# A four-layer graph network on one core: d added on TensorE for two tiles of five, norms ended on ScalarE, one scale product on GpSimd, and a new table of places

## The chip, the core and the metric

The kernel runs on one core of a Trainium2 chip. The core has TensorE (PE, matrix products into PSUM), VectorE (DVE), ScalarE (ACT), GpSimd (POOL) and SyncE (SP, which here issues the DMAs). Each engine runs its own instructions in the order in which they were issued; semaphores between the engines keep the dependencies. The metric is the device time of one execution, in microseconds (us).

## The reference

There are 64 graphs of 256 nodes with 128 features, and a 0/1 adjacency matrix for each. Four layers follow one another, each as x = layernorm(x + layer(x, adj)):

```python
# layer 0: p = x @ (W1 - W2), q = x @ W2
x0 = max over j of relu(p_i + q_j + b) * adj[i, j]
# layer 1: three elu projections, two aggregations adj @ . and adj.T @ ., tanh update
# layer 2: a graph convolution with normalised adjacency, elu between its products
# layer 3, for every edge i, j:
pre = m_j + m_i + b1                    # m_j = x @ W1[:D], m_i = x @ W1[D:]
msg = gelu(layernorm(pre) * g1 + be1)
agg_i = sum over j of msg * adj[i, j]
updated = layernorm(concat(x, agg) @ W2 + b2) * g2 + be2
```

Layer 3 is the large one: a normalised, gated message for each edge.

## The kernel before, in words

**Sparse edges as columns.** The kernel sorts the nodes of a graph by their number of neighbours and lays the neighbours out in 40 slots (`RECTS`). Slot s is a block of columns, one for each node that may have an s-th neighbour; all slots together are `WIDTH` = 4800 columns for each half of the nodes. `hot` is a 0/1 matrix (fp8) that picks for every column which of the half's 128 nodes is its neighbour, so that one product `c3 x hot` on TensorE gathers the neighbours' part of the message into columns. The features are split into three bf16 parts (`split3`), hence three products for each block of 512 columns.

**Tiles of layer 3.** `TILES` cuts the 4800 columns of a half into four tiles of 1024 columns and one of 704; with both halves there are ten tiles in a graph (`TODO`). Tiles 0 to 2 hold whole slots of 256 columns. For each tile `sums_of` (L855) does the following. TensorE makes blocks of 512 columns in PSUM. VectorE adds the receiving node's part `dT`, repeated for every slot, and writes `pre` in SBUF. ScalarE squares `pre` into `sq`, TensorE sums the squares over the partitions with a matrix of ones, ScalarE scales them into `row`. A DMA writes the row to a `line` in DRAM; for two tiles at a time, it is read back as 128 x 16 (`vr`), GpSimd raises it to the power -1/2 and multiplies it by the mask `fu`, and DMAs write it to DRAM and spread it over all partitions (`rs_s`). `last` (L960) then multiplies `pre` by `rs_s` on VectorE, applies Gelu with scale and bias on ScalarE, and adds the tile to `sums` on VectorE (`fold`). A product with a part of W2 follows for each half, and `update` (L436) adds, normalises and stores. `sums_of` runs four tiles ahead of `last` (`AHEAD`); `pre` has 7 buffers, `rs_s` 3, `sq` 1.

**Norms.** `layernorm` (L296) is used five times in a graph: at the end of layers 0, 1 and 2 (x1, x2, x3), for y of layer 3, and for the output. VectorE takes mean and variance (`bn_stats`, `bn_aggr`), GpSimd adds epsilon and raises to -1/2 (`rs`, two instructions), and VectorE ends it: for each half one `tensor_scalar` (subtract the mean, multiply by rs), or, with gamma and beta, two `scalar_tensor_tensor`. In layers 0 to 2 TensorE transposes the result next.

**Order.** Nothing in the program is a loop on the chip. A tape (`Tape`, L86) records the instructions of each graph, in four parts (`first`, `second`, `third`, `last`). `AT` gives each of the 665 recorded instructions of a graph a place, and graph g stands g x `PERIOD` later; all instructions of all graphs are issued in the order of `AT[i] + g * PERIOD`. So several graphs are in work at once, and an engine meets their instructions in the order that the table gives, not in the order in which their inputs become ready. `BANKS` gives the PSUM bank of each of the 82 PSUM tiles of a graph. In the profile almost every instruction has line L117, the place where the tape plays it, so groups are told apart by tile names.

Of the kernel before, what the change touches and what calls it, by code (L numbers as in the profile page):

```python
# [9 lines left out]
F32 = mybir.dt.float32  # L10
# [18 lines left out]
for _s0, _n, _w in RECTS:  # L29
# [10 lines left out]
PERIOD = 68597  # L40
AT = [
    0, 17760, 60075, 113136, 105182, 105182, 105183, 102831, 102831, 102831, 110669, 110669, 110669, 110669,
    106819, 106819, 106819, 106819, 132589, 112770, 113194, 113191, 114149, 114680, 115572, 116600, 127108, 127385,
    127477, 127638, 128456, 128456, 128456, 128456, 129252, 167352, 167352, 167352, 167352, 170028, 167469, 167469,
    167469, 167469, 169266, 129252, 129869, 138338, 138338, 175384, 175384, 175384, 175384, 185704, 188498, 198206,
    138877, 158428, 163223, 205266, 194576, 218329, 202165, 190466, 198713, 197410, 172321, 133325, 134073, 132100,
    134755, 130433, 131857, 138013, 130475, 132679, 141029, 136544, 147371, 141091, 138254, 149904, 142022, 143828,
    134350, 136963, 130888, 154057, 152143, 136812, 131597, 135682, 150302, 50267, 50267, 51142, 106173, 106173,
    110809, 113092, 114103, 115412, 142716, 142716, 142716, 142716, 142716, 138772, 138772, 138772, 138772, 138772,
    146600, 143243, 143243, 143243, 143243, 143243, 148201, 146140, 146140, 146140, 146140, 146140, 150206, 145880,  # L50
    145880, 145880, 145880, 145880, 151986, 151684, 151684, 151684, 151684, 151684, 152911, 152448, 152448, 152448,
    152448, 152448, 156338, 153971, 153971, 153971, 153971, 153971, 153971, 153971, 153971, 157134, 157697, 157805,
    157380, 157380, 157380, 157380, 157380, 157380, 157380, 157380, 158172, 158547, 160090, 143916, 143916, 143916,
    143916, 157893, 161048, 162139, 172702, 172702, 172702, 161211, 161211, 161211, 161211, 165106, 163675, 163675,
    163675, 163675, 163675, 165268, 165091, 165091, 165091, 165091, 165091, 166836, 165893, 165893, 165893, 165893,
    165893, 167925, 166285, 166285, 166285, 166285, 166285, 168867, 150182, 150182, 150182, 150182, 150182, 170700,
    170268, 170268, 170268, 170268, 170268, 171887, 172059, 172059, 172059, 172059, 172059, 172059, 172059, 172059,
    173999, 174804, 175613, 174543, 174543, 174543, 174543, 174543, 174543, 174543, 174543, 176934, 178826, 179479,
    163756, 163756, 163756, 163756, 164398, 179873, 180116, 180116, 180116, 182699, 182699, 182699, 182699, 182699,
    182699, 182699, 182699, 182699, 182699, 182699, 182699, 182699, 182699, 182699, 182699, 182699, 184638, 186829,  # L60
    188393, 190261, 192462, 189659, 192419, 192462, 192463, 193382, 193799, 194283, 194283, 196229, 197739, 197739,
    197863, 199404, 199404, 199767, 196229, 196269, 196428, 198141, 203643, 204759, 204759, 204759, 204759, 204759,
    207105, 207105, 207105, 207105, 207105, 207105, 209069, 209905, 209982, 211997, 213309, 211020, 212716, 216020,
    216021, 216021, 216021, 138164, 164455, 180398, 183224, 195565, 216021, 216021, 216232, 217871, 217871, 219655,
    220859, 221353, 222845, 224313, 225709, 225758, 226367, 227329, 227329, 227329, 227329, 227488, 229896, 229896,
    230186, 230112, 230186, 232038, 233437, 234508, 235780, 235780, 235780, 235780, 235780, 237440, 238099, 238099,
    238277, 238100, 239978, 240898, 243374, 241359, 243047, 244102, 247526, 247526, 248324, 188591, 248522, 248522,
    248522, 249117, 249117, 252769, 251596, 251704, 253761, 254891, 252769, 252769, 252769, 252769, 256816, 257931,
    257931, 257931, 257931, 256055, 256055, 256055, 256994, 258732, 260232, 260232, 260232, 260232, 260803, 260803,
    259203, 259203, 259203, 260422, 259088, 259088, 259088, 259089, 260678, 261279, 261279, 261279, 261279, 261442,  # L70
    261696, 270059, 272065, 277752, 279128, 279128, 261244, 261244, 261244, 261305, 260228, 260228, 260228, 260814,
    261622, 262731, 262731, 262731, 262731, 266778, 275218, 263270, 263270, 263270, 265037, 259210, 259210, 259210,
    261433, 263668, 268962, 270855, 270855, 270855, 270855, 271063, 277538, 279564, 285260, 296203, 296203, 296203,
    281115, 285903, 260489, 260489, 260489, 270476, 264721, 266934, 268118, 268118, 268118, 271078, 272421, 274438,
    274438, 274438, 274438, 280012, 286089, 283767, 291651, 298416, 268002, 268002, 268002, 271712, 268406, 268406,
    268406, 273881, 277066, 281788, 281788, 281788, 281788, 282305, 292280, 296324, 283720, 296324, 301082, 308174,
    285903, 292378, 303270, 266792, 266792, 266792, 269082, 269338, 269338, 269338, 271169, 282084, 284789, 284789,
    284789, 284789, 288190, 302392, 300082, 305371, 310143, 296586, 292360, 292360, 292360, 296407, 290067, 290067,
    290067, 295222, 296579, 298916, 298916, 298916, 298916, 299552, 306172, 309408, 304155, 309648, 314896, 315843,
    305620, 308455, 311827, 306236, 301007, 301007, 301007, 302221, 296040, 296040, 296040, 301658, 297892, 306172,  # L80
    308294, 308294, 308294, 308294, 308659, 310486, 315715, 316106, 317663, 313660, 317279, 318829, 305328, 305328,
    305328, 309145, 308304, 308057, 304348, 304348, 304348, 308422, 313472, 314786, 314786, 314786, 314786, 314858,
    317455, 319233, 325254, 326737, 326737, 327338, 319719, 321478, 324328, 320137, 320749, 323171, 320164, 327517,
    331173, 331173, 331173, 331173, 331173, 331173, 331173, 331173, 331173, 331173, 331173, 331173, 331173, 323787,
    324347, 327390, 324328, 329258, 327518, 324432, 329492, 329598, 330030, 330250, 331498, 331262, 332381, 333437,
    333711, 335099, 336414, 335343, 337991, 342336, 342336, 342336, 342336, 342336, 342336, 342336, 342336, 342336,  # L86
    342336, 342336, 342336, 342337, 350509, 350509, 350509, 350509, 350509, 350509, 350509, 350509, 350509, 350509,
    354346, 357521, 365298, 358477, 367762, 370480, 370480, 372624, 382049, 380501, 380733, 384069, 386653, 390490,
    389663, 400076, 408707, 408708, 420847, 415132, 436409,
]  # L90
BANKS = [
    3, 0, 0, 5, 0, 4, 2, 7, 1, 7, 5, 4, 3, 5, 7, 0, 2, 7, 3, 0, 5, 1, 4, 3, 7, 0, 3, 1, 6, 7, 1, 2, 5, 6, 2, 2, 4,
    6, 7, 2, 3, 5, 7, 4, 7, 0, 3, 1, 3, 6, 0, 2, 4, 1, 0, 6, 5, 1, 5, 7, 4, 3, 0, 4, 1, 6, 0, 2, 5, 4, 2, 4, 0, 2,
    1, 1, 3, 5, 6, 4, 3, 6,
# [73 lines left out]
def kernel(  # L168
# [118 lines left out]
    class Shared:  # L287
# [8 lines left out]
        def layernorm(self, dst, src, at, g=None, be=None):  # L296

            st = self.work.tile([P, H, 6], F32, name="st_" + at, bufs=2)
            mv = self.work.tile([P, H, 2], F32, name="mv_" + at, bufs=2)
            for h in range(H):  # L300
                nc.vector.bn_stats(st[:, h], src[:, h])
                nc.vector.bn_aggr(mv[:, h], st[:, h])
            rs = self.work.tile([P, H], F32, name="rs_" + at, bufs=2)
            nc.gpsimd.tensor_scalar(rs, mv[:, :, 1], EPS, 1.0, ALU.add, ALU.mult)
            inverse_root(rs)
            yield
            for h in range(H):
                if g is None:
                    nc.vector.tensor_scalar(
                        dst[:, h], src[:, h], mv[:, h, 0:1], rs[:, h:h + 1], ALU.subtract, ALU.mult  # L310
                    )
                else:
                    nc.vector.scalar_tensor_tensor(dst[:, h], src[:, h], mv[:, h, 0:1], g, ALU.subtract, ALU.mult)
                    nc.vector.scalar_tensor_tensor(dst[:, h], dst[:, h], rs[:, h:h + 1], be, ALU.mult, ALU.add)
# [159 lines left out]
    def sparse(ctx):  # L474
# [306 lines left out]
        def layer_0(s):  # L781
# [66 lines left out]
            yield from sh.layernorm(s["x1"], y, "0")  # L848

        TODO = [(h, t0, tl) for h in range(H) for t0, tl in TILES]  # L850
        AHEAD = 4
        GROUP = 2
        PIECE = 16

# [428 lines left out]
```

## Time and profile before

| | |
|---|---|
| time, median of 3 runs | 4605.34 us (4604.03 to 4610.56) |
| the profiled execution's own time | 4603.78 us |
| its span | 4601.9 us |
| granted TensorE clock, mean | 0.957 |
| DMA | 365.10 MB, mean 79 GB/s |
| square of `pre` on ScalarE, 128x1024 | 512 times, 1052 ns |
| sums over slots on VectorE, 128x1024 | 256 times, 1213 ns |
| power of `vr` on GpSimd, 128x16 | 192 times, 2942 ns |

How to read it: PE is TensorE's matmuls, PEld its weight loads, which overlap them. "x" with a number is a count of instructions. A group's row has the tile that is written, the tiles that are read, the forms, the count, the busy time in us, the mean length of one in ns, and after the second bar the idle time ahead of these instructions on their engine with what ended it. Busy times of overlapping instructions are counted once, so busy divided by count can be less than the mean length. In the windows view, each row has the start, end and length of a stretch and each engine's busy time in it. In the view of waits a row is: the waiting engine and tile, what it waited for, total us, times, longest. In the chain and the timeline the first two numbers are start and length in us.

### The profile page before, as it was taken

The numbers are of one execution on the slowest core, as the hardware profiler recorded it, in microseconds if no ns is written. First come the engines' busy times: TensorE is split into PE (matmuls) and PEld (weight loads), VectorE is DVE, ScalarE is ACT, GpSimd is POOL, SyncE is SP. The second block draws the span as 40 slices with busy tenths as digits, with TensorE's granted clock in tenths as the row PEclk, the third lists the DMA queues.
The fourth block names the chain that finished last, engine by engine and source line by source line (L and its number), as shares of the span: only waits on it lengthen the run. The fifth ranks groups of instructions, "written<-read, shape, count | busy, mean of one in ns | idle before, by whom it ended". The sixth has DMA issues, their size and how long they took to land.

```text
span 4601.9 us, 83551 instructions
## 1 busy us (share of the span) xinstructions
PE 4000.7 (87%) x28434; PEld 2519.0 (55%) x28434; DVE 4467.9 (97%) x12373; ACT 2967.6 (64%) x4862; POOL 1848.6 (40%) x1674
## 2 busy tenths in 40 slices
PE   4889889889889888898898898898888988988985
PEld 2555555555555555555555555555555555555553
DVE  6999999999999999999999999999999999999997
ACT  2666666666666666666666666666666666666664
POOL 0344343434444444443444434444444434344443
PEclk9999999999999999999999999999999999999997
DMA  1122222222222222222222222222222222222222
GB/s 28 62 84 77 82 81 80 76 89 81 77 80 80 85 77 85 85 77 82 80 81 76 89 81 76 81 80 84 81 81 85 77 82 80 81 76 89 78 72 94
DMA packets 292663, 365.10 MB, mean 79 GB/s; under 512 B 151936, under 2 KB 210304, under 8 KB 292224
## 3 DMA queue, kind: packets, MB, share of 16 engines
q1 hardware_dynamic: 292224, 359.66, 24.5%
q8 instruction: 225, 3.69, 0.3%
q14 instruction: 214, 1.75, 0.1%
HBM read 345.00 MB, written 14.53 MB: 78 GB/s over the span
## 4 chain that ended last, share of the span: by engine, by line
DVE 62%; PE 28%; issue 7%; ACT 2%; DMA 1%; POOL 1%; SPq 0%; DVEq 0%; POOLq 0%; ACTq 0%
PE ps L117 28%; DVE pre L117 18%; DVE lanes L117 12%; DVE sums L117 10%; DVE hot L117 4%; DVE hs L117 3%; DVE x L117 2%; DVE st L117 2%; DVE z L117 2%; DVE io L117 2%; DVE perm L117 1%; DVE elu_hs L117 1%; DVE mv L117 1%; DVE total_m L117 1%; ACT row L117 1%
## 5 line engine op out<-in xcount | busy, mean ns | idle before, releaser
L117 POOL TENSOR_TENSOR vr<-vr,mhalf 128x16 f32<-128x16 f32 (+1 forms) x320 | 994.3, 3107 | 451.0 <-DMA vr<-line 451.0
L117 PE MATMUL ps<-hot,q 128*128 128x512 fp8e4 (+1 forms) x3840 | 922.8, 365 | 58.6 <-ACT row L117 52.9
L117 POOL TENSOR_SCALAR rs<-mv 128x2 f32<-128x2 f32 x256 | 134.4, 525 | 2003.4 <-DVE mv L117 2003.3
L117 PE MATMUL ps<-hot,c 128*128 128x512 fp8e4 (+1 forms) x3840 | 892.1, 366 | 0.9 <-ACT row L117 0.9
L117 DVE TENSOR_TENSOR pre<-ps,dT 128x512 f32<-128x512 f32 (+6 forms) x1664 | 857.4, 532 | 6.1 <-PE ps L117 2.7
L117 ACT ACTIVATE sq<-pre 128x1024 f32<-128x1024 f32 (+1 forms) x640 | 640.1, 1000 | 336.4 <-DVE pre L117 282.4
L117 DVE TENSOR_TENSOR lanes<-ps,lanes 128x512 f32<-128x512 f32 (+6 forms) x1536 | 767.1, 499 | 3.5 <-ACT lanes L117 1.0
L117 DVE TENSOR_TENSOR pre<-pre,rs_s 128x1024 f32<-128x1024 f32 (+1 forms) x640 | 734.7, 1148 | 10.3 <-DMA rs_s<-scale_line 10.2
L117 ACT ACTIVATE pre<-pre,be,g 128x1024 f32<-128x1024 f32 (+1 forms) x512 | 600.5, 1173 | 105.3 <-DVE pre L117 101.3
L117 DVE TENSOR_TENSOR sums<-pre,sums 128x1024 f32<-128x1024 f32 (+6 forms) x1024 | 631.0, 616 | 0.4 <-ACT pre L117 0.2
L117 PEld LDWEIGHTS <-c 128*128 128x128 bf16 x3840 | 353.2, 98 | 347.7 <-issue 70.2
L117 DVE TENSOR_SCALAR hot<-rank 128x512 fp8e4<-128x512 bf16 (+5 forms) x1536 | 503.5, 355 | 1.5 <-ACT rank L117 1.4
L117 PEld LDWEIGHTS <-q 128*128 128x128 bf16 x3840 | 322.3, 97 | 300.5 <-issue 94.6
L117 PE MATMUL ps<-sq,ones 128*32 128x256 f32 (+1 forms) x5120 | 392.7, 378 | 54.2 <-ACT sq L117 51.7
L117 PEld LDWEIGHTS <-pick 128*128 128x128 bf16 x2944 | 240.1, 97 | 258.3 <-issue 1.4
L117 ACT ACTIVATE row<-ps,eps_t 128x256 f32<-128x256 f32 (+1 forms) x640 | 290.8, 454 | 126.3 <-PE ps L117 124.5
L117 ACT ACT_TABLE_LOAD x253 | 324.6, 1283 | 22.6 <-DVE w3c L117 18.2
L117 PE MATMUL ps<-w3u,sums 128*128 128x128 f32 x2048 | 287.4, 287 | 28.3 <-DVE sums L117 17.1
L117 PE MATMUL ps<-ident,x 128*128 128x128 f32 x512 | 137.5, 325 | 198.2 <-DVE x L117 189.5
L117 PEld LDWEIGHTS ps<-w3u,sums 128*128 128x128 f32 x2048 | 251.7, 193 | 80.1 <-DVE pre L117 36.2
L117 PE MATMUL ps<-lack,pick 128*128 128x6 bf16 (+16 forms) x2944 | 266.1, 185 | 0.0
L117 POOL TENSOR_TENSOR rs<-rs,mhalf 128x2 f32<-128x2 f32 x256 | 249.8, 976 | 16.1
(230 smaller groups left out, 7357.0 us busy)
## 6 DMA issues: line engine op xcount, KB each, us to landing
rs_s<-scale_line SPq DMA_DIRECT2D x512, 512.0 KB
rs_s<-scale_line SPq DMA_DIRECT2D x128, 352.0 KB
an<-in_adj SPq DMA_DIRECT2D x64, 256.0 KB
x<-in_x SPq DMA_DIRECT2D x64, 128.0 KB
line<-row SPq DMA_DIRECT2D x512, 4.0 KB
out<-o SPq DMA_DIRECT2D x64, 128.0 KB
vr<-line SPq DMA_DIRECT2D x192, 8.0 KB
fu<-fulls SPq DMA_DIRECT2D x192, 4.0 KB
```

The source lines that it names most:

```text
L117: getattr(getattr(self.nc, engine), op)(*args, **named)
```

## The change

- For tiles 1 and 2 of each half (`OWN`), d is added on TensorE: after the three products of a 512 block, four transposing products with `dk` as stationary matrix and the identity as moving one are accumulated into the same bank. ScalarE then copies the bank to `pre`, where VectorE added before. `dk` is the transpose of `dT`, made once for each graph by four transposes and one ScalarE copy.
- For tile 3 of each half (`SLOW`) the product `pre` times `rs_s` is on GpSimd instead of VectorE.
- `layernorm` ends on ScalarE: GpSimd makes `off` = -mean x rs in two instructions, and for each half one Identity activation with scale rs and bias off follows. The form with gamma and beta is gone: for y of layer 3, VectorE multiplies by gamma (one 128x256 product), and beta is added to x3 beforehand on GpSimd (`x3b`).
- `AT` has 712 places for 712 instructions, `BANKS` 83, and `PERIOD` is 76270 instead of 68597.

```diff
-PERIOD = 68597
+PERIOD = 76270
...
-        def layernorm(self, dst, src, at, g=None, be=None):
+        def layernorm(self, dst, src, at):
...
             for h in range(H):
-                if g is None:
-                    nc.vector.tensor_scalar(
-                        dst[:, h], src[:, h], mv[:, h, 0:1], rs[:, h:h + 1], ALU.subtract, ALU.mult
-                    )
-                else:
-                    nc.vector.scalar_tensor_tensor(dst[:, h], src[:, h], mv[:, h, 0:1], g, ALU.subtract, ALU.mult)
-                    nc.vector.scalar_tensor_tensor(dst[:, h], dst[:, h], rs[:, h:h + 1], be, ALU.mult, ALU.add)
+            off = self.work.tile([P, H], F32, name="off_" + at, bufs=2)
+            nc.gpsimd.tensor_tensor(off, mv[:, :, 0], rs, ALU.mult)
+            nc.gpsimd.tensor_scalar(off, off, -1.0, 0.0, ALU.mult, ALU.add)
+            yield
+            for h in range(H):
+                nc.scalar.activation(
+                    dst[:, h], src[:, h], AF.Identity, bias=off[:, h:h + 1], scale=rs[:, h:h + 1]
+                )
...
+            x3b = self.work.tile([P, H, P], F32, name="x3b")
+            nc.gpsimd.tensor_tensor(x3b, x3, over_halves(be3u), ALU.add)
...
-            yield from self.layernorm(z, y, "3", g3u, be3u)
-            nc.vector.tensor_add(z, z, x3)
+            yield from self.layernorm(z, y, "3")
+            nc.vector.tensor_mul(z, z, over_halves(g3u))
+            nc.vector.tensor_add(z, z, x3b)
...
+        OWN = (TILE, 2 * TILE)
+        SLOW = (3 * TILE,)
...
                     nc.tensor.matmul(
-                        pt[:, :bl], c3[:, k, h], hot[:, h, t0 + b:t0 + b + bl], start=k == 0, stop=k == 2
-                    )
+                        pt[:, :bl], c3[:, k, h], hot[:, h, t0 + b:t0 + b + bl],
+                        start=k == 0, stop=k == 2 and not own,
+                    )
+                if own:
+                    for o in range(0, 512, P):
+                        nc.tensor.matmul(
+                            pt[:, o:o + P], dk[:, h, o // P % H], ident, start=False, stop=o + P == 512,
+                            is_transpose=True,
+                        )
+                    nc.scalar.copy(pre[:, b:b + 512], pt)
+                    continue
...
+            pk = psum()
+            for h in range(H):
+                for hk in range(H):
+                    cols = slice((h * H + hk) * P, (h * H + hk + 1) * P)
+                    nc.tensor.transpose(pk[:, cols], dT[:, h, hk * P:(hk + 1) * P], ident)
+            dk = state.tile([P, H, H, P], F32, name="dk")
+            nc.scalar.copy(dk.rearrange("p a b d -> p (a b d)"), pk)
...
-                    nc.vector.tensor_mul(pre[:, :tl], pre[:, :tl], rs[:, :tl])
+                    if t0 in SLOW:
+                        nc.gpsimd.tensor_tensor(pre[:, :tl], pre[:, :tl], rs[:, :tl], ALU.mult)
+                    else:
+                        nc.vector.tensor_mul(pre[:, :tl], pre[:, :tl], rs[:, :tl])
```

The two tables are left out of this diff. Where each instruction falls on its engine follows from sorting the places modulo the period.

## The prediction, made before the changed kernel ran

> **What bounds the kernel now.** I read the page's busy shares and its chain first, then a stretch of the steady state, then single groups. Busy shares and chain:
>
> ```profile
> PE 4000.7 (87%) x28434; PEld 2519.0 (55%) x28434; DVE 4467.9 (97%) x12373; ACT 2967.6 (64%) x4862; POOL 1848.6 (40%) x1674
> DVE 62%; PE 28%; issue 7%; ACT 2%; DMA 1%; POOL 1%; SPq 0%; DVEq 0%; POOLq 0%; ACTq 0%
> ```
>
> VectorE (DVE) is nearly full, but TensorE (PE) stands close behind it. The windows of the middle, and one piece of the chain that returns with every graph:
>
> ```profile
> core 0: us, PE busy (x) PEld busy (x) DVE busy (x) ACT busy (x) POOL busy (x), PEclk, DMA share, GB/s
> 1700.00:2400.00 700.00, 621.55 (x4445) 391.62 (x4444) 692.44 (x1911) 463.87 (x760) 288.74 (x261) 0.96 0.26 81
> 2040.11 11.48 PE ps L117 x99
> 2180.06 11.48 PE ps L117 x99
> ```
>
> Two graphs take 2180.06 - 2040.11 = 139.95, so one takes 69.98 us. Of this DVE is busy 69.24 (98.9%), PE 62.16, ScalarE (ACT) 46.4, GpSimd (POOL) 28.9. 64 x 69.98 = 4479 of the span of 4601.9; the other 123 are filling and draining. The profiled execution took 4603.8, the median of the runs is 4605.3; I work on 4603.8.
>
> **DVE, per graph.** The groups by form that lose work, and the one nearest to what is added:
>
> ```profile
> L117 DVE TENSOR_TENSOR pre<-pre,rs_s 128x1024 f32<-128x1024 f32 x512 | 621.9, 1215 | 10.3 <-DMA rs_s<-scale_line 10.2
> L117 DVE TENSOR_TENSOR pre<-ps,dT 128x512 f32<-128x512 f32 x896 | 598.5, 681 | 5.7 <-PE ps L117 2.7 <-ACT sums L117 1.6 <-ACT dT L117 1.2
> L117 DVE TENSOR_SCALAR x<-hs,mv,rs 128x128 f32<-128x128 f32 x128 | 96.5, 754 | 0.0
> L117 DVE TENSOR_SCALAR x<-y,mv,rs 128x128 f32<-128x128 f32 x256 | 77.0, 344 | 6.6 <-POOL rs L117 1.9
> L117 DVE SCALAR_TENSOR_TENSOR z<-z,rs,be3u 128x128 f32<-128x128 f32 x128 | 43.0, 338 | 1.0 <-POOL rs L117 0.8
> L117 DVE SCALAR_TENSOR_TENSOR z<-y,mv,g3u 128x128 f32<-128x128 f32 x128 | 41.7, 326 | 0.0
> L117 DVE TENSOR_SCALAR o<-z,mv_o,rs_o 128x128 f32<-128x128 f32 x128 | 41.1, 323 | 1.1 <-POOL rs_o L117 1.1
> L117 DVE TENSOR_TENSOR z<-z,x 128x256 f32<-128x256 f32 x64 | 27.2, 424 | 0.0
> ```
>
> I divide the busy column by 64 graphs. The d additions: 8 of 14 are gone, 598.5 x 8/14 / 64 = 5.34. The scale products of the fourth tile: 2 of 8, 621.9 / 4 / 64 = 2.43. The norms' ends: (96.5 + 77.0 + 43.0 + 41.7 + 41.1) / 64 = 4.68. Added is one product by gamma, 27.2 / 64 = 0.42. DVE: 69.24 - 12.45 + 0.42 = 57.2 us. The old end of layer 2's norm shows that POOL can hold it up:
>
> ```profile
> 2009.89 1.15 POOL L117 TENSOR_TENSOR diff<-an,nz 128x512 bf16<-128x512 f32 x1
> 2009.91 1.22 DVE L117 TENSOR_SCALAR x<-hs,mv,rs 128x128 f32<-128x128 f32 x1
> 2011.17 0.33 DVE L117 TENSOR_SCALAR x<-hs,mv,rs 128x128 f32<-128x128 f32 x1
> ```
>
> The same instruction takes 0.33 alone and 1.22 beside a POOL product: 0.89 of the 1.15 is lost. The new products are twice as long, 2 x 1.157 = 2.3 us, twice per graph. [...] I take 0.77 (0.89/1.15) of it, 3.6, since sums and products with two inputs fill much of that stretch: DVE 60.8. Either way (57.2 to 61.8) it is no longer the fullest.
>
> **PE.** Added are 32 transposes that add d and 4 that make dk. Rows of the same instruction with the same operands' shape (layer 2 adds hs so):
>
> ```profile
> 2058.66 0.81 PE L117 MATMUL ps<-aT,hs 128*128 128x256 f32 x3
> 2059.30 0.38 PE L117 MATMUL ps<-ident,hs 128*128 128x128 f32 x2
> 2059.52 0.81 PE L117 MATMUL ps<-hot,c 128*128 128x512 fp8e4 x3
> ```
>
> Two of them hold PE for 2059.52 - 2059.30 = 0.22, so 0.11 each: 36 x 0.11 = 4.0 us. The group's busy time (48.9 us for 256) would say 0.19, or 6.9. [...] The rows' 273 ns is a duration with its pipeline latency in it, not a distance; I take 0.11. Weight loads hide behind the matmul before (PEld 55%). PE: 62.2 + 4.0 = 66.1. [...]
>
> **ACT.** The rows to price from:
>
> ```profile
> L117 ACT COPY lanes<-ps 128x512 f32<-128x512 f32 x128 | 73.2, 572 | 15.5 <-DVE total_m L117 9.1 <-PE ps L117 6.4
> L117 ACT ACTIVATE pre<-pre,be,g 128x1024 f32<-128x1024 f32 x384 | 475.8, 1239 | 11.6 <-DVE pre L117 10.6
> L117 ACT ACT_TABLE_LOAD x253 | 324.6, 1283 | 22.6 <-DVE w3c L117 18.2
> ```
>
> Nine copies of 128x512 (eight d blocks, one dk): 9 x 0.57 = 5.1. Ten norm ends of 128x128 with both scale and bias from memory: Gelu at 1024 takes 1239 and at 704 takes 974, so 0.83 ns an element and 0.39 fixed, 0.50 at 128; a 128x176 row takes 0.41. I take 0.45: 4.5. The table of places puts Gelu, Tanh and Exp in another order: sorted modulo its period there are six changes between Gelu and the others, where the old table has four (253 / 64), so 2 x 1.28 = 2.6. ACT: 46.4 + 12.2 = 58.6.
>
> **POOL and queues.** Two products 4.6, five "off" products at 0.71 (the row dinv by pos), five negations at 0.52 (rs from mv), x3b 0.6 (half of diff): 28.9 + 11.4 = 40. No bound, but order matters: POOL's second product now stands right before layer 0's rs, and waits for its scale DMA; rs, and behind it ACT's norm end and PE's transposes of x1, wait with it. DMAs are the same in number and size; only SP's order is new. x3b costs nothing while POOL idles; in a full POOL it would be its 0.6.
>
> **Sum.** Fullest is now PE, 66.1, against 69.98: at most 3.9 us a graph to gain. What PE still waits for decides. Today:
>
> ```profile
> PE ps L117 <- DVE x L117: 189.5, 129, 3.4
> PE ps L117 <- DVE hs L117: 107.6, 248, 2.2
> ```
>
> With the smaller ones that name DVE (pre 23.2, total_m 20.7, sums 17.1, io 13.9, perm 13.2) this is 385 us, 6.0 a graph; waits that name ACT (row 53.7, sq 51.7, nzp 22.9, x3T 17.1) are 145, 2.3 a graph. A DVE at 60.8 of 68 no longer has a standing queue, so I drop the 6.0 and keep ACT's 2.3: 66.1 + 2.3 = 68.4 a graph. Filling and draining get longer by five norms of 1.4 (below) and dk, 8 us. 4603.8 - 64 x 1.6 + 8 = 4509; I say **4510**, with 4440 to 4590 for this case alone.
>
> **Rivals.**
> - *PE never waits* (14%). 66.1 a graph: 4603.8 - 64 x 3.9 + 8 = 4362. For it: DVE and ACT both under 61. Against: three engines now stand within 8 us of each other and all run in a fixed order.
> - *The norm is the new wait* (30%, slower). A norm's end was POOL 0.52 + 0.98, then DVE. Now POOL does two more instructions (0.71 + 0.52), and ACT takes it 0.2 slower than DVE: 1.4 longer; behind it in ACT's order stand the copies that free PSUM. POOL's rs takes 0.19 to 1.33 today, depending on DVE, so the added pair may cost 0.4 to 2.6. x1, x2 and x3 stand before PE: 3 x 1.4 = 4.2 a graph if the new order puts no other PE work there. 66.1 + 2.3 + 4.2 = 72.6: 4603.8 + 64 x 2.6 + 8 = 4778. It decides once PE idles over 3.9 us a graph. If the old 3.0 for x stays beside it, 75.6 and 4971. For it: waiting for x is PE's largest wait already.
> - *Transposes cost their busy time or more* (14%, slower). [...] Against: the distances above.
> - *Same* (6%): PE's idle is just the 3.9.
> [...]
>
> The new table's period of 76.27, against 68.60, I don't read as a time: only the order that follows from it runs. But it spaces work for slack that the engines may not need, and that keeps some weight on the slow side.
>
> **Numbers.** Forecast 36%, PE without waits 14%: faster 0.50; same (within 0.2%, about what a measurement can tell) 0.06; slower 0.44. The range of 8 in 10 runs from the fast rival's 4362, rounded up to 4370, over the slow one's 4778 to 4880, near the 4895 of dear transposes; beyond lie the doubled norm wait and a PE fuller than I think.
>
> **What would show it.** Right: DVE near 60 a graph, PE about 66 and over 95% of the period, transposes 0.11 apart, six table loads a graph, PE's waits under 3 a graph. Wrong: PE waiting for x through ACT for more than 3.9 a graph; POOL's vr or rs standing behind a product; transposes 0.2 or more apart; DVE instructions of over 2 us beside POOL's products.

## The result, and the profile after

The changed kernel takes 4796.0 us (4777.97 to 4798.18, 4 runs) against 4605.6 of the kernel before in the same session: a ratio of 1.040, 95% interval 1.038 to 1.043. It is slower by 190 us, or 3.0 us a graph; 4510 had been forecast. Its profiled execution has a span of 4796.4 and a mean granted clock of 0.962. Busy shares and chain of its page:

```profile
PE 4179.4 (87%) x30738; PEld 2738.3 (57%) x30738; DVE 4292.0 (89%) x11029; ACT 3604.4 (75%) x6204; POOL 2335.7 (49%) x2506
DVE 36%; PE 27%; POOL 13%; issue 10%; ACT 9%; DMA 4%; SPq 0%; POOLq 0%; DVEq 0%; ACTq 0%
```

No engine is as full as DVE was (97%), and yet the kernel takes longer. POOL, ACT and DMA, which together held 4% of the chain, hold 26% of it now: the end is set by a chain that hops between engines. The windows of the middle, and two pieces of the chain that lie four graphs apart:

```profile
1700.00:2400.00 700.00, 614.71 (x4610) 404.12 (x4608) 644.03 (x1632) 539.04 (x929) 349.28 (x371) 0.98 0.25 77
1933.59 13.23 PE ps L120 x103
2226.33 13.23 PE ps L120 x103
```

A graph takes (2226.33 - 1933.59) / 4 = 73.2 us, where 68.4 had been forecast. (Four graphs are a small sample: from output to output over the middle 45 graphs it is 72.8.) Of it PE is busy 614.71 / 700 x 73.2 = 64.3, DVE 67.3, ACT 56.4, POOL 36.5. So PE stands idle for 8.9 us a graph, where 2.3 had been forecast. Its largest waits:

```profile
PE ps L120 <- ACT sq L120: 193.7, 137, 2.8
PE ps L120 <- DVE dg L120: 118.2, 58, 2.2
PE ps L120 <- DVE pre L120: 59.3, 113, 2.1
PE ps L120 <- DVE total_m L120: 49.3, 63, 1.0
PE ps L120 <- ACT x L120: 46.3, 65, 4.7
PE ps L120 <- DVE hs L120: 35.7, 79, 1.6
```

The wait for x, the largest before (189.5), is small now; the waits for `sq` and for the tile `dg` of layer 2 have taken its place. Summed over the whole view, PE waits 596 us; before it was 584. PE's busy time, which is 179 us longer (4000.7 to 4179.4), thus comes on top of waits that did not fall: together that is nearly the whole 190. The groups that bear on the steps of the prediction:

```profile
L120 ACT ACT_TABLE_LOAD x379 | 486.3, 1283 | 24.8 <-DVE w3c L120 18.1
L120 POOL TENSOR_TENSOR pre<-pre,rs_s 128x1024 f32<-128x1024 f32 x128 | 306.1, 2391 | 278.3 <-DMA rs_s<-scale_line 231.1 <-ACT perm_f L120 47.3
L120 ACT COPY pre<-ps 128x512 f32<-128x512 f32 x512 | 286.5, 580 | 20.3 <-PE ps L120 20.3
L120 DVE TENSOR_SCALAR elu_hs<-elu_hs 128x256 f32<-128x256 f32 x192 | 135.4, 705 | 1.4 <-ACT elu_hs L120 1.4
L120 DVE TENSOR_TENSOR sums<-pre,sums 128x284 f32<-128x284 f32 x128 | 113.7, 888 | 2.4
L120 DVE TENSOR_TENSOR z<-z,x3b 128x256 f32<-128x256 f32 x64 | 82.7, 1292 | 6.7
L120 POOL TENSOR_TENSOR off<-mv,rs 128x2 f32<-128x2 f32 x256 | 63.4, 247 | 20.1
L120 ACT ACTIVATE x<-hs,off,rs 128x128 f32<-128x128 f32 x128 | 56.2, 487 | 10.2 <-POOL off L120 4.7
L120 DVE TENSOR_TENSOR z<-z,g3u 128x256 f32<-128x256 f32 x64 | 27.2, 425 | 145.5 <-ACT z L120 145.5
```

Prices are mostly as forecast: 379 / 64 = 5.9 table loads a graph, a copy 0.58, a norm's end 0.49, a product on POOL 2.39. The last row is not: DVE stands idle 145.5 us ahead of y's product by gamma, until ACT has made z.

### The profile page after: what moved, and what is told of

Read it like the earlier page. It is cut to its first block, busy times and chain, and to the rows that moved or that the text cites. A ratio compares the mean times of both kernels' runs of the same rounds, so it can differ in the third digit from the quotient of the medians.

```text
span 4796.4 us, 88740 instructions
## 1 busy us (share of the span) xinstructions
PE 4179.4 (87%) x30738; PEld 2738.3 (57%) x30738; DVE 4292.0 (89%) x11029; ACT 3604.4 (75%) x6204; POOL 2335.7 (49%) x2506
## 4 chain that ended last, share of the span: by engine, by line
DVE 36%; PE 27%; POOL 13%; issue 10%; ACT 9%; DMA 4%; SPq 0%; POOLq 0%; DVEq 0%; ACTq 0%
PE ps L120 27%; DVE pre L120 8%; DVE sums L120 7%; POOL vr L120 7%; DVE lanes L120 6%; POOL rs L120 3%; DVE hs L120 3%; DMA vr<-line 2%; ACT sq L120 2%; DVE hot L120 2%; POOL dinv L120 1%; POOL off L120 1%; ACT pre L120 1%; ACT row L120 1%; DMA line<-row 1%
## 5 line engine op out<-in xcount | busy, mean ns | idle before, releaser
L120 POOL TENSOR_TENSOR vr<-vr,mhalf 128x16 f32<-128x16 f32 (+1 forms) x320 | 1008.4, 3151 | 1425.4 <-DMA vr<-line 1331.1
L120 PE MATMUL ps<-hot,c 128*128 128x512 fp8e4 (+1 forms) x3840 | 1017.7, 381 | 132.8 <-DVE dg L120 118.2
L120 PE MATMUL ps<-hot,q 128*128 128x512 fp8e4 (+1 forms) x3840 | 960.5, 375 | 35.4 <-DVE pre L120 32.8
L120 DVE TENSOR_TENSOR sums<-pre,sums 128x1024 f32<-128x1024 f32 (+6 forms) x1024 | 707.3, 691 | 16.9 <-ACT pre L120 2.7
L120 DVE TENSOR_TENSOR pre<-pre,rs_s 128x1024 f32<-128x1024 f32 (+1 forms) x512 | 577.9, 1137 | 30.9 <-DMA rs_s<-scale_line 30.6
L120 PE MATMUL ps<-sq,ones 128*32 128x256 f32 (+1 forms) x5120 | 407.6, 391 | 193.7 <-ACT sq L120 193.7
L120 DVE TENSOR_TENSOR pre<-ps,dT 128x512 f32<-128x512 f32 (+6 forms) x1152 | 512.4, 466 | 24.3 <-PE ps L120 24.2
L120 POOL TENSOR_TENSOR pre<-pre,rs_s 128x1024 f32<-128x1024 f32 x128 | 306.1, 2391 | 278.3 <-DMA rs_s<-scale_line 231.1
L120 PEld LDWEIGHTS ps<-ident,dk 128*128 128x128 f32 x2048 | 269.3, 147 | 109.0 <-issue 16.8
L120 PE MATMUL ps<-ident,dk 128*128 128x128 f32 x2048 | 322.7, 282 | 0.0
L120 ACT COPY pre<-ps 128x512 f32<-128x512 f32 x512 | 286.5, 580 | 20.3 <-PE ps L120 20.3
```

What stands on the lines that cost most here:

```text
L120: getattr(getattr(self.nc, engine), op)(*args, **named)
```

## The experiments

Sixteen variants ran on a chip, in the groups in which they stand here, each in three rounds beside the kernel before. "The old order" is the table of places and the bank numbers of before; an instruction that it does not know stands beside the one that it replaces (`off` after rs, the transposes after the third product of their block, the copy where the addition stood). "The new order" is the table of the change; an instruction put back stands where its replacement stood. The first four expectations name two theories. A: it is where the new order puts things, above all the power of `vr` on POOL ahead of the norms' rs. B: it is the moved work itself, POOL's product with its stalls above all. (The expectations call these port stalls; the runs show how long DVE is held beside the product, 2.79 us for 0.71 in the stretch below, and not by what.)

**The whole work of the change in the old order.**

```diff
-PERIOD = 76270
+PERIOD = 68597
```

> All of the changed kernel's work, but in the order of the table before: each replaced instruction keeps the old place, each added one takes the place of its neighbour. Theory A (the new table's order loses the time, the moved work itself relieves VectorE as forecast): at or under the 4605 of before, about 4510. Theory B (the moved work costs the time whatever the order: longer norms and port stalls): 4700 or more.

Measured: 4729.4, ratio 1.027 (1.025 to 1.028). Of the 190, 124 come with the work even in the order of before, 67 with the new order.

**The work of before in the new order** (the opposite pairing: that table and its period under the instructions of before).

> The work of the kernel before (d on VectorE, norms ended on VectorE, no product on GpSimd) in the new table's order; the places of instructions that do not exist stay empty. Theory A: the order alone costs, with VectorE fuller than in the changed kernel on top, so 4800 or more. Theory B: near before, 4600 to 4650.

Measured: 5007.4, ratio 1.088 (1.086 to 1.089). The new order suits only the work that it was laid out for. With this work it costs 402, so the split into 124 and 67 above holds only for taking the work first and the order second.

**The power of the second pair of tiles later.** The power, its product with `fu` and the two DMAs that follow go behind the norms of layers 3 and 1 (the four places that change, in the table).

```diff
-305585, 305585, 314366, 315975    # vr to the power, vr x fu, scale_line, rs_s
+317165, 317166, 317170, 317171
```

> The changed kernel with one GpSimd pair moved: the power and mask of the second pair of tiles stand behind the norm instructions of layers 3 and 1 that they stood ahead of, with the two DMAs that follow from them. Theory A in its narrow form (the norms wait in GpSimd's queue behind a power that waits for its DMA): 2 us a graph or more come back, 4660 or less. If that queue is not what decides: 4796 within 0.5%.

Measured: 5090.0, ratio 1.105 (1.103 to 1.107), much slower. DVE then waits for the scale instead:

```profile
DVE pre L117 <- DMA rs_s<-scale_line: 504.6, 80, 9.3
```

In the changed kernel that row has 30.6. The total that theory A expected does not come, but its mechanism shows: DVE's wait for z falls from 145.5 to 5.4, so y's norm did stand behind the power, and PE's wait for `sq` falls from 193.7 to 51.9. The edit delays the scale as well, and loses there more than it gains. So the power can't simply give way, and this run does not settle what the norm's wait behind it costs.

**The fourth tile's product back on VectorE, new order.**

```diff
-        SLOW = (3 * TILE,)
+        SLOW = ()
```

> The changed kernel with the fourth tile's scale product back on VectorE, same table. VectorE gets 2 x 1.21 = 2.4 us a graph more of its own work and loses the stalls behind two GpSimd products. If these stalls decide (Theory B, ports): 4700 or less. If order decides: 4796 within 0.5%, or up to 4900 if VectorE is what the chain runs through.

Measured: 4711.0, ratio 1.023 (1.021 to 1.025). POOL's product costs 85. This stretch of the changed kernel shows how:

```profile
2024.39 2.49 POOL L120 TENSOR_TENSOR pre<-pre,rs_s 128x1024 f32<-128x1024 f32 x1 [3.95 <-DMA rs_s<-scale_line]
2024.40 2.79 DVE L120 TENSOR_TENSOR sums<-pre,sums 128x108 f32<-128x108 f32 x2
2027.12 0.16 DVE L120 TENSOR_TENSOR viol<-viol,fl 128x9 f32<-128x9 f32 x1
...
2027.66 1.27 DVE L120 TENSOR_TENSOR pre<-ps,dT 128x512 f32<-128x512 f32 x2
2028.86 0.14 DVE L120 TENSOR_REDUCE dg<-ps 128x2 f32<-128x4 f32 x1
...
2029.05 0.81 PE L120 MATMUL ps<-hot,c 128*128 128x512 fp8e4 x3 [1.98 <-DVE dg L120]
```

The product starts at 2024.39. Two sums on DVE, which take 0.26 + 0.45 alone by the rows of before, need 2.79 and end 0.3 after it. What follows on DVE is late by 2 us, `dg` among it, and PE waits 1.98 for `dg`. Without the product PE no longer waits for `dg` (118.2 in the changed kernel). Its wait for `hs` rises from 35.7 to 85.7 instead, so that its waits fall by only 31 us in sum.

**One part at a time in the old order.** These four split the 124. Three parts were taken alone, then two together.

TensorE's addition of d alone: the `OWN` part of the change, with norms and products of before.

> The order of before with one part of the change alone: d is added on TensorE for tiles 1 and 2 and copied by ScalarE; norms end on VectorE and all products are on VectorE, as before. VectorE loses 5.3 us a graph (69.2 to 63.9), TensorE gains 4.0 (62.2 to 66.1), ScalarE 5.1. Theory 1 (the cost of the change sits in GpSimd's product and in the norm's way over GpSimd and ScalarE; the TensorE add is sound): a graph takes about 68.4 to 69, so 4500 to 4560 us, faster than before. Theory 2 (the extra transposes and copies are the cost: TensorE's banks come free later through ScalarE): 4640 to 4720, and the other parts alone are near 4605.

Measured: 4714.4, ratio 1.024 (1.022 to 1.026). Not the gain that theory 1 wanted. DVE falls from 4468 to 4213, PE rises from 4001 to 4222, and PE's first wait is as long as before (189.5):

```profile
PE ps L123 <- DVE x L123: 190.6, 68, 3.4
```

One of these waits for x, with what DVE does ahead of it:

```profile
2049.68 0.78 POOL L123 TENSOR_TENSOR rs<-rs,mhalf 128x2 f32<-128x2 f32 x1
...
2050.78 0.41 DVE L123 TENSOR_TENSOR z<-z,x 128x256 f32<-128x256 f32 x1
...
2051.11 1.84 DVE L123 TENSOR_TENSOR pre<-pre,rs_s 128x704 f32<-128x704 f32 x1
...
2052.88 0.33 DVE L123 TENSOR_TENSOR lanes<-ps,lanes 128x180 f32<-128x180 f32 x1
...
2053.13 0.33 DVE L123 TENSOR_SCALAR x<-hs,mv,rs 128x128 f32<-128x128 f32 x1
...
2053.52 0.84 PE L123 MATMUL ps<-ident,x 128*128 128x128 f32 x2 [2.94 <-DVE x L123]
```

rs is there at 2050.46, but x stands in DVE's order behind other instructions and starts at 2053.13. Over the whole trace DVE is busy in 99% of the time in which PE waits for x, though it is busy in only 89% of the span; in the waits of over 1 us (189 us together) 155 us lie between the end of rs and the start of x. So this is a queue on DVE, at this place of the order, and less work elsewhere does not shorten it.

The norms' end on ScalarE alone: the `layernorm` part of the change with `x3b`.

> The order of before with the norms' end alone moved: GpSimd makes off in two instructions, ScalarE ends the norm, beta of the last norm is added beforehand on GpSimd; d and all products stay on VectorE. VectorE loses 4.3 us a graph. Theory 1: the norm's way is longer by 1.4 us or more for each of x1, x2, x3, and TensorE waits for x; 4605 plus 60 to 150, so 4660 to 4750. Theory 2: the norm costs nothing, VectorE's relief comes through: 4450 to 4600.

Measured: 4507.9, ratio 0.979 (0.978 to 0.981), a gain of 97. Theory 1 was wrong on the norm, in the old order. PE's waits fall by 105 us in sum (584 to 479). That for x stays, now through two other engines:

```profile
PE ps L123 <- ACT x L123: 171.2, 130, 4.1
```

```profile
2028.79 1.14 POOL L123 TENSOR_TENSOR rs<-rs,mhalf 128x2 f32<-128x2 f32 x1
...
2030.00 0.92 POOL L123 TENSOR_TENSOR off<-mv,rs 128x2 f32<-128x2 f32 x1
...
2030.90 0.97 ACT L123 ACTIVATE pre<-pre,be,g 128x704 f32<-128x704 f32 x1 [1.02 <-DVE pre L123]
2031.01 0.19 POOL L123 TENSOR_SCALAR off<-off 128x2 f32<-128x2 f32 x1
...
2031.78 0.48 ACT L123 ACTIVATE x<-hs,off,rs 128x128 f32<-128x128 f32 x1
...
2032.31 0.47 PE L123 MATMUL ps<-ident,x 128*128 128x128 f32 x1 [2.36 <-ACT x L123]
```

Of the waits of over 1 us (158 together) 80 us pass between rs and the finished `off` on POOL, and 37 more until ACT, which does a Gelu first, starts x.

POOL's product alone: `SLOW` as in the change.

> The order of before with the fourth tile's scale product on GpSimd alone. VectorE loses 2.4 us a graph of work and gains stalls beside GpSimd's two products of 2.4. Theory 1: 4605 plus 40 to 100, so 4640 to 4700, since VectorE is the bound here and loses more in stalls than the product took. Theory 2: within 30 of 4605.

Measured: 4804.0, ratio 1.045 (1.043 to 1.047). It costs 199, more than the expected 100: DVE's busy time doesn't fall at all (4468 to 4531), since the stalls give back the work that is gone, and its waits double (115 to 239).

All but the product:

> The order of before with the TensorE add and the norms' end on ScalarE, and every scale product on VectorE: all of the change but GpSimd's product, in the old order (the whole work in that order took 4729). If GpSimd's product costs what it cost in the new order (85): 4644. If it costs nothing in the old order, where VectorE has slack: 4729. Under theory 1 it is also slower than the TensorE add alone by the norm's 60 to 150; under theory 2 it is near it.

Measured: 4722.0, ratio 1.025 (1.024 to 1.027). It takes 8 more than TensorE's addition alone: once that is in, the norm's gain is lost, and the product's price (7, up to 4729) too. In the old order TensorE's addition sets the time: PE has 60% of the chain of this kernel, where it had 28% before.

**Why: transposes or copies?** Both on top of the norms' end in the old order (4508). The first keeps the transposes but lets DVE add as before; the second keeps the copies but leaves the transposes for d out.

```diff
-                    nc.scalar.copy(pre[:, b:b + 512], pt)
-                    continue
```

> The order of before with the norms' end on ScalarE (4508 for that alone), plus TensorE's 36 transposes a graph for tiles 1 and 2, but no ScalarE copy of the blocks: VectorE still adds d, so d is in twice. It is the transposes' price by themselves. Theory P (TensorE's chain of work and fixed waits sets the end, so its added 4.0 us a graph come through one to one): 4508 plus 180 to 260, about 4720. Theory C (the price of the TensorE add is the copy through ScalarE, which frees the bank later): 4510 to 4560.

```diff
-                    for o in range(0, 512, P):
-                        nc.tensor.matmul(
...
-                        )
                     nc.scalar.copy(pre[:, b:b + 512], pt)
```

> The same base, with ScalarE's copies of tiles 1 and 2 in place of VectorE's additions, but without the 32 transposes that add d (d is left out for these tiles; the 4 transposes and the copy for dk stay). Theory P: VectorE is relieved by 5.3 us a graph and TensorE hardly loaded, so 4400 to 4530, at or below 4508. Theory C: 4650 to 4720, nearly all of the 214 between the norm alone (4508) and norm and TensorE add (4722).

Measured: 4653.5 (ratio 1.011, 1.009 to 1.012) and 4525.7 (0.982, 0.981 to 0.984). So the transposes alone cost 146 of the 214, the copies alone 18; the remaining 50 come only with both. In the first, PE's busy time is 221 us longer than in the norms' kernel (4003.6 to 4224.9) and its waits are 76 us shorter. The copies' kernel tells more. Its DVE has 270 us less to do than the norms' kernel (4056 against 4327), its ACT 270 more (3472 against 3202), and it is not faster:

```profile
PE ps L123 <- ACT x L123: 179.2, 130, 4.1
PE ps L123 <- ACT sq L123: 131.7, 198, 2.4
```

The wait for x stays (171.2 in the norms' kernel), and that for `sq` rises from 42.2. Freeing DVE by loading ACT gains nothing there; what freeing DVE alone would gain no run shows. PE with waits that stay sets the end, and most of its added work comes on top.

**Parts in the new order.** First the norms' end alone, as the only part of the change.

> The new order with the norms' end on ScalarE alone; d and all products on VectorE (the work of before in this order took 5007, the norm and the TensorE add together 4711). If the new order leans on the moved d additions, because it was laid out for a lighter VectorE: 4880 to 4990. If the norm was what it needed: 4711 or less.

Measured: 4906.0, ratio 1.065 (1.063 to 1.067): again about 100 less than without it (5007). TensorE's addition on top of it (4711) gains 195 here, where it cost 214 in the old order. The traces say how: here PE's waits fall by 319 us (884 to 565) and its busy time grows by 117 (4010.2 to 4127.3); in the old order the waits fall by only 46 (479 to 432) and the busy time grows by 264 (4003.6 to 4268.0). Then the changed kernel with all five norms back on DVE:

> The changed kernel as it is, new order too, with one part undone: norms end on VectorE again, without off and without beta added beforehand. My rival of before (the norm's way over GpSimd and ScalarE is the new wait, 4.2 us a graph): it takes most of the loss back, 4560 to 4680. Theory 3 (from the old order, where the norm's end on ScalarE was a gain of 97): it gets slower, 4830 to 4950.

Measured: 4730.8, ratio 1.027 (1.026 to 1.029). Neither fits: the norm costs 65 here, a quarter of my rival's 4.2 us a graph (269 us), and not the gain of theory 3. That left the question which norm.

**Which norm.** In the changed kernel only y of layer 3 goes back to DVE, with gamma and beta, and `x3b` goes; x1, x2, x3 and the output keep their end on ScalarE.

```diff
-            yield from self.layernorm(z, y, "3")
-            nc.vector.tensor_mul(z, z, over_halves(g3u))
-            nc.vector.tensor_add(z, z, x3b)
+            yield from self.layernorm(z, y, "3", g3u, be3u)
+            nc.vector.tensor_add(z, z, x3)
```

> The changed kernel with one of its five norms undone: y of layer 3 ends on VectorE with gamma and beta, and beta is not added beforehand; x1, x2, x3 and the output still end on ScalarE. With all five back the time fell by 65 (4796 to 4731). Theory Z (the norm's price in the new order is VectorE standing 2.3 us a graph for z through GpSimd and ScalarE, and z's addition running 1.35 us beside GpSimd): 4700 to 4745. Theory X (my rival: x1, x2, x3 ahead of TensorE): 4780 to 4800, nothing comes back.

Measured: 4630.7, ratio 1.006 (1.004 to 1.007). One norm of five costs 165, and the other four gain 100 (4731 to 4631). Theory X is out. The changed kernel around z:

```profile
2059.34 0.78 POOL L120 TENSOR_TENSOR rs<-rs,mhalf 128x2 f32<-128x2 f32 x1
2060.20 0.20 POOL L120 TENSOR_TENSOR off<-mv,rs 128x2 f32<-128x2 f32 x1
2060.49 0.19 POOL L120 TENSOR_SCALAR off<-off 128x2 f32<-128x2 f32 x1
2060.71 0.49 ACT L120 ACTIVATE z<-y,off,rs 128x128 f32<-128x128 f32 x1 [2.82 <-POOL off L120]
...
2061.11 0.45 ACT L120 ACTIVATE row<-ps,eps_t 128x256 f32<-128x256 f32 x1
2061.47 0.48 ACT L120 ACTIVATE z<-y,off,rs 128x128 f32<-128x128 f32 x1
2061.85 1.04 ACT L120 ACTIVATE sq<-pre 128x1024 f32<-128x1024 f32 x1
...
2061.98 0.42 DVE L120 TENSOR_TENSOR z<-z,g3u 128x256 f32<-128x256 f32 x1 [2.43 <-ACT z L120]
...
2062.43 1.16 POOL L120 TENSOR_TENSOR diff<-an,nz 128x512 bf16<-128x512 f32 x1
2062.51 1.35 DVE L120 TENSOR_TENSOR z<-z,x3b 128x256 f32<-128x256 f32 x1
...
2062.95 0.64 PE L120 MATMUL ps<-sq,ones 128*32 128x256 f32 x8 [2.13 <-ACT sq L120]
```

From the end of rs (2060.12) to the end of z's addition (2063.86) it takes 3.74 us. ACT stands idle 2.82 for `off`, with `row` and `sq` queued behind, and PE then waits 2.13 for `sq`; DVE stands idle 2.43; the addition then runs beside `diff` and takes 1.35 instead of 0.42. The same place with y's norm on DVE:

```profile
2052.77 1.70 POOL L123 TENSOR_TENSOR rs<-rs,mhalf 128x2 f32<-128x2 f32 x1
...
2054.03 0.34 DVE L123 SCALAR_TENSOR_TENSOR z<-y,mv,g3u 128x128 f32<-128x128 f32 x1
2054.50 0.61 DVE L123 SCALAR_TENSOR_TENSOR z<-z,rs,be3u 128x128 f32<-128x128 f32 x2
...
2055.14 0.42 DVE L123 TENSOR_TENSOR z<-z,x 128x256 f32<-128x256 f32 x1
```

From rs (2054.47) to the sum (2055.56) it takes 1.09. (From the start of rs it is 4.52 against 2.79, since rs itself takes 0.78 there and 1.70 here.) Half of DVE's instructions need only the mean and run before rs is there. PE's wait for `sq` falls from 193.7 to 68 in this kernel, but that for `pre` rises from 59.3 to 146.6.

**Do the prices add?** The same, with the product back on DVE too (`SLOW = ()`); then TensorE's addition alone in the new order.

> The same, and the fourth tile's scale product back on VectorE too (that alone gave 85). If the two prices add: 4796 - 85 - 65, about 4646. If both were the same lateness of VectorE's queue: 4700.

> The new order with the TensorE add alone, all norms and all products on VectorE. If the prices of the product (85) and of the norm (65) add: about 4646. In the old order the TensorE add alone took 4714. If VectorE's load decides here: 4720 to 4780.

Measured: 4496.8 (ratio 0.978, 0.976 to 0.980) and 4631.7 (1.006, 1.004 to 1.007). The first is the fastest of all, 109 under the kernel before. The product costs 134 here, against 85 beside the late z; y's norm costs 214 without the product, 165 with it. 134 + 214 = 348, of which the changed kernel shows 299 (4796 - 4497): the two overlap by 49. The norms of x1, x2, x3 and the output together gain 135 (4632 to 4497).

PE's time in these kernels, which all have the same 30738 matmuls in the same order, tells in what form the prices are paid (the last three columns are of the profiled execution):

| | time | PE busy | PE waits | granted clock |
|---|---|---|---|---|
| the changed kernel | 4796 | 4179 | 596 | 0.962 |
| product back on DVE | 4711 | 4127 | 565 | 0.968 |
| y's norm back on DVE | 4631 | 4068 | 555 | 0.983 |
| both back | 4497 | 4032 | 440 | 0.990 |

Only half of the 299 is shorter waiting (156); the other half (148) is PE's busy time. Busy time times clock is 3991 to 4021 in all four, so most of that half goes with the clock (4179 x 0.962 / 0.990 = 4061, which is 118 of the 148). Why the clock is higher in the faster kernels is not shown; no run changes it by itself.

**Four norms in the old order.**

> The order of before with four of the five norms ending on ScalarE and y's on VectorE (all five there: 4508). VectorE does 1.0 us a graph more (26.2, 29.4 and the addition against four instructions of 43.0 + 41.7). If VectorE's load sets the end there: 4508 plus 40 to 65, about 4560. If the gain came from x2's end no longer meeting GpSimd's diff (52 of the 97) and TensorE's chain sets the end: 4500 to 4520.

Measured: 4505.2, ratio 0.979 (0.977 to 0.980), the same as with five (4508). There y's norm is neither gain nor loss: DVE waits for its z 3 us in all. In that order the sum comes 13 us after rs with either form of the norm (12.6 with all five norms on ScalarE, 13.3 here, medians of the middle graphs), so a few us more on the way are hidden; in the new order it comes 3.7 us after rs, and nothing hides them. So the size of the price is not in the instructions but in who stands behind them, and how soon. That four norms are as good as five also means that DVE's load alone did not set the end there.

## Why the prediction was wrong

**The step that failed** is "A DVE at 60.8 of 68 no longer has a standing queue, so I drop the 6.0 and keep ACT's 2.3". It takes the queue from DVE's average load. I dropped 385 us of waits that name DVE and kept 145 that name ACT; in the changed kernel PE waits 316 us for DVE and 259 for ACT. What an average hides is the place: PE's waits hang on a few results, and what stands ahead of these in the fixed order stays when DVE has less to do elsewhere. With TensorE's addition alone DVE is busy 89% of the span and PE waits for x 190.6 us, as before, with DVE busy in 99% of that time. With the norms' end alone x no longer waits on DVE, and PE still waits 171 us for it, now for the steps on POOL and ACT. In the changed kernel PE waits 8.9 us a graph, 6.6 more than I kept. PE's busy time came out 1.8 lower (64.3 for 66.1, at a clock of 0.98 in that stretch, where the stretch of before had 0.96), and 6.6 - 1.8 = 4.8 is the miss of the sample, 73.2 against 68.4 (with the 72.8 of 45 graphs it is 4.4; the time missed by 286 us, 4.5 a graph). The fastest kernel of this study keeps 440 us of PE waits, against 596. That its 4497 lies near the 4510 that I forecast for the whole change is luck: it has fewer parts, longer waits than the forecast and less busy time.

**What filled the waits** is two parts of the change. y's norm I priced at 1.4 us of extra length and put under filling and draining; it takes 2.65 more from rs on (3.74 against 1.09), and ACT and DVE both stand in order behind it: 165 to 214 us of time, part of it at a lower clock. POOL's product I priced by DVE's stalls alone; that DVE's lateness comes back as PE's wait for `dg` I had not followed. It costs 85 to 134.

**Step by step:**
- *Transposes:* right. In one stretch of the changed kernel:

```profile
2029.70 0.60 PE L120 MATMUL ps<-ident,dk 128*128 128x128 f32 x4
2030.13 0.81 PE L120 MATMUL ps<-hot,c 128*128 128x512 fp8e4 x3
```

  Four hold PE for 0.43, so 0.108 each, while the rows of all 2048 have a mean length of 282 ns and overlap. The 4895 of dear transposes, near which the range of the prediction ends, asks for more than twice this distance and rests on no run: of the 1536 distances from one such transpose to the next in the changed kernel the median is 0.109 and the longest 0.214. In the old order with TensorE's addition alone PE's busy time grew by 221 us, 3.5 a graph for 4.0 (at a clock of 0.949 for 0.957; elsewhere by 117 and 264, as above). But 0.11 is not free where PE's waits stay: alone they cost 146 us, 2.3 a graph.
- *DVE's stalls:* the size was right, the sum was not. For instructions with two inputs I took the 0.77 that a row with one input had lost, an estimate; no run shows that share for them, nor the whole 4.6 behind the 61.8. What the runs showed in its place: eight groups (those of three DVE rows above, `viol`, the maxima of `lanes`, `sums` of 108, `place` and `hot` of 72) got longer by 303 us, 4.7 a graph; with the product back on DVE only 90 of it are left, so the product makes 213, or 3.3 for my 3.6. Neighbouring DVE rows overlap, though: added up by group they make 5364.6 in the kernel before, where DVE's busy time is 4467.9, 72 ns for each of 12373 instructions. I took row lengths off the busy time, so 1344 instructions fewer gave 97 us too much. In the changed kernel, where DVE waits more, the overlap is also smaller (57 ns for each of 11029). Hence 67.3 a graph and not 60.8.
- *DVE as the bound of before:* half right. Moving the norms' end gained 97 in the old order, but 270 us more relief, paid for with ACT's time, gained nothing (the copies' kernel).
- *ACT:* 56.4 for 58.6, the six loads as read from the table. *POOL:* 36.5 for 40; `off` took 0.25 and 0.24, not 0.71 and 0.52. As loads neither bound; what they cost came through the order (above).
- *POOL's order:* I watched the second product ahead of layer 0's rs. What stood ahead of y's rs was the power of `vr`, 3.29 on average, and its wait for a DMA grew from 451.0 to 1331.1.
- *The rival "the norm is the new wait"* gave 4778, 18 from the result, for a wrong reason, so by luck: x1, x2, x3 and the output together gain by the move. The norm that cost was y's, and the product made up the rest.
- *The new order:* 67 slower than the old one for the full change, as measured; for the fastest version only the new order was tried. That the addition on TensorE gains 195 in the one and costs 214 in the other is PE's waits, of which it removes 319 us in the one and 46 in the other. Why the new order holds such waits stays open: no run varied single places beyond the power's.
- *Sums:* busy time a graph was taken over 70.0 us (62.16 and 69.24); over 69.98 it is 62.14 and 69.22. Of the 6.0 us of waits, 0.3 (`sums`, 17.1 us in two pieces) is not paid in every graph. Neither changes the forecast.

## What to carry to other kernels

Don't drop a wait because the engine that it names has less to do on average. Look at the place: what stands ahead of the awaited instruction in the order, and is it work of that engine or a chain of short steps over several? Here PE's largest wait outlived DVE's relief in both forms, and most of the work added to PE came on top. A move of the same instruction can gain in four places and lose more in a fifth: price each place by who stands in order behind it, on the engine that it leaves and on the one that it enters. Undo a change of several parts one part at a time; here two of them hid a version that is 2.2% faster than the kernel before.

## What the runs showed of the hardware

- A product of 128x1024 on POOL took 2.39 us on average in the changed kernel. Of the `sums` on DVE (two inputs in SBUF) that began within one, all 27 of 128x284 ended 0.31 us after it, and 7 of 9 of 128x108 ended 0.12 to 0.13 after it; the other two began in its first 0.02 us and took 0.27, as alone. Of the two in the row above, 2.79 us for 0.71 together, the one of 128x284 was held. Additions with an input in PSUM were not held: 47 rows `pre<-ps,dT` of 128x512 that lay wholly within such a product (the kernel with the product alone) took 0.681 us, the others 0.678. A scalar operation with one input was hit as well: `elu_hs` went from 281 to 705 ns on average, and back to 285 without the product. What holds DVE there no run shows. The product's stalls came to 3.3 us a graph, where the two products take 2 x 2.39 = 4.8.
- The granted clock did not follow the transposes. In the old order it went from 0.957 to 0.949 with 2304 of them more (TensorE's addition alone), stayed at 0.948 with them on top of the norms' end, and was 0.956 with the transposes but no copies; in the fastest kernel, which has them, it was 0.990. With the same matmuls in the same order PE's busy time went with the clock: 4179 us at 0.962, 4032 at 0.990.
- DVE's rows overlapped with the next one by some 70 ns while it was full and by 57 in the changed kernel, so its busy time is no fixed sum of row lengths: those of before add up to 20% more.
